# One denominator product per attention half instead of two, in a four-layer graph network on one core

## Chip, core and metric

The kernel runs on one core of a Trainium2 chip. The metric is the device time of one launch in microseconds (us). The kernel before has a median of 4019.16 us over three runs (4017.57 to 4020.96).

## What is computed

There are 16 graphs of 1024 nodes with 256 features, and one 1024x1024 adjacency matrix for all. Each graph goes through three graph-attention layers (4, 1 and 1 heads) and then one transformer block with 8 masked attention heads of width 32 and a feed-forward part. The change touches the attention of the last layer only, cut here to what matters:

```python
def _L3_gnn_ref(x, adj, w_qkv, ...):
    qkv = jnp.einsum('fnc,ck->fnk', x, w_qkv)
    q, k, v = jnp.split(qkv, 3, axis=-1)          # then 8 heads of 32
    scores = jnp.einsum('fnhd,fmhd->fhnm', q, k) / sqrt(32)
    scores = jnp.where(adj > 0, scores, -1e9)
    attn = jax.nn.softmax(scores, axis=-1)
    t = jnp.einsum('fhnm,fmhd->fnhd', attn, v).reshape(F, N, C)
    ...
```

The kernel makes the softmax without a maximum: weight = exp(score) times a 0/1 mask. The numerator is the product of weights and values, the denominator is the sum of the weights over m, and the quotient of the two is the result.

## The kernel before, in words

**Attention of one graph** (function `attention`, lines 1138 to 1461). The 8 heads come in two groups g of four, and the 1024 queries in two halves hf of 512. So a graph has four pairs (g, hf), called attention halves here. Each half has eight steps jt, one for each tile of 128 keys. A step does the following.

- TensorE computes four score tiles of 128 keys x 512 queries, one for each head (line 1417). They land in a ring of four PSUM tiles `sc`.
- ScalarE takes the exponential of each (line 1441) into two tiles `pa` of 128x1024, two heads in each. The ring `pa` has six tiles, which is three steps.
- VectorE multiplies each `pa` tile by the mask (line 1450).
- TensorE multiplies the values by the weights, four heads side by side in four 32-column strips of the array (`quad`, line 1274, called at line 1324). The result accumulates over the eight steps in a PSUM bank, `accs[g, hf][0]`.

**The denominator.** The same `quad` with a tile of ones in place of the values gives the sum over keys, in a second bank `accs[g, hf][1]` (line 1339). To spare TensorE, the weights of several steps are first added elementwise into two tiles `sums` (a ring of two, so one set). With a run of four steps this goes so: at the second step VectorE adds the weights of the first two (line 1301); at the third an accumulating transfer, issued from GpSimd, adds its weights into `sums` (line 1318); at the fourth VectorE adds again (line 1309), and then comes the product of ones. A half thus has two products of ones. In the last graph the run is one: each step has its own product of ones, and nothing is added beforehand.

After the eighth step ScalarE copies both banks (line 1357), TensorE transposes them back, and VectorE divides (lines 1377 to 1397). The four PSUM banks of `r_bank` are shared by all stages; a use gets its bank with its first instruction.

**What orders the work.** Nothing is run as it is written. Every operation is recorded with an assumed duration, the buffers that it reads and writes, and a key. The key comes from the graph's number and from a curve (`KNOTS`) for its stage, moved for some engines by `LEAD`. `Record.schedule` (lines 193 to 310) then fills each engine's queue: of the operations that it takes to be ready it takes the one with the least key, with a surcharge `BIAS` times `SWITCH` for a TensorE operation that changes between the full array and the 32-column strips. `PASS` and `SLACK` are its allowances for the hand-over between engines and for a transfer's landing. The result is a fixed order on each engine. The stages of neighbouring graphs lie interleaved in it: while one graph is in its attention, the next is in its graph layers, whose largest parts are the products at line 951 (full array), at lines 1038 and 1048 (32-column strips) and their weights on VectorE (line 924).

Each engine works through its own order and waits there for what an instruction needs. The transfers that SyncE issues (keys, queries, rows, inputs, outputs) are one queue; the adding transfers are in GpSimd's order, together with its small power operations for the layer norms (lines 499 and 514) and its running sums (lines 544 and 875).

Of the kernel before, what the change touches and what calls it, by code (L numbers as in the profile page):

```python
# [113 lines left out]


WEIGHT = {"pe": 1.0, "dve": 0.3}
PASS = {"pe": 0.156, "act": 0.266, "dve": 0.175, "pool": 0.13, "dma": 0.0}


class Port(float):  # L120
# [3 lines left out]
class Work:  # L124


    def __init__(self, engine, us, emit, key, modes, moved, lands):
        self.engine, self.us, self.emit, self.key, self.modes = engine, us, emit, key, modes
        self.pass_on = PASS[engine]
        self.moved = moved  # L130
# [9 lines left out]
def priority(x):  # L140
# [3 lines left out]
    key = base + knots[k] + (knots[k + 1] - knots[k]) * (at - k)  # L144
    return round(key - (LEAD.get(x.engine, 0.0) if lead else 0.0), 6)


class Record:
# [44 lines left out]
    def schedule(self):  # L193
        for n, x in enumerate(self.work):
# [4 lines left out]
            for y in x.before:  # L199
                y.after.append(x)  # L200
        free = dict.fromkeys(PASS, 0.0)
        queue = 0.0
        future = {e: [] for e in PASS}
        now = {e: [] for e in PASS}
        mode = "full"
# [15 lines left out]
        def turn(x):  # L221

            return BIAS * SWITCH.get((mode, x.modes[0]), 0.0) if x.engine == "pe" else 0.0

        def choose(e):

            at = free[e]
            while future[e] and future[e][0][0] <= at:
                x = heapq.heappop(future[e])[2]
                heapq.heappush(now[e], (x.key, x.n, x))  # L230
            best = None
            for key, n, x in now[e]:
                t = opening(x)
                if t is not None:
                    best = min(best or (1e9,), (max(at, t), key + turn(x), n, x))
            if future[e] and (best is None or future[e][0][0] < best[0]):
                for t, n, x in sorted(future[e]):
                    if opening(x) is not None:
                        t = max(t, at, opening(x))
                        best = min(best or (1e9,), (t, x.key + turn(x), n, x))  # L240
                        break
            return best
# [15 lines left out]
        while True:  # L258
            choices = [(c, e) for c, e in ((choose(e), e) for e in PASS) if c]
            if not choices:  # L260
# [30 lines left out]
            if x.moved:  # L291
                if e == "dma" and queue - at > BEHIND:
                    us = max(us, HELD)
                queue = max(at + (us if e == "pool" else 0.2), queue) + x.moved
                x.pass_on = queue + x.lands + SLACK - (at + us)
            order.append(x)
# [14 lines left out]


BEHIND, HELD = 2.0, 1.35
SLACK = 0.748
KNOTS = {
    "gat0": (-11.844, -10.615, -6.023, -6.927, -4.773, -4.496, -2.083, -5.225, -6.038),
    "gat1": (-1.994, -0.279, 0.283, 0.497, 0.692, 0.622, 0.809, 0.954, 0.61),
    "gat2": (1.323, -0.293, -0.231, 0.287, 0.727, 1.303, 1.532, 1.921, 1.614),
    "beside": (1.385, 3.608, 5.021, -2.136, 7.34),
    "values": (-1.057, -3.755, -2.847, -3.057, -2.059, -1.343, 5.264, -0.6, 1.007),  # L320
    "steps": (-0.497, 1.051, 1.31, 1.573, 1.666, 1.995, 2.455, 2.56, -0.935),
    "feed": (3.891, 3.879, 2.109, 1.26, 2.247, 1.635, -2.072, 2.278, 2.962),
    "last": (3.265, -3.949, 2.052, -2.131, 3.084, -1.607, -0.666, 3.92, 2.042),
}
BIAS = 3.411
LEAD = {"act": 1.749, "dve": -1.422}

SWITCH = {
    ("full", "col4"): 0.137,
# [11 lines left out]
def tt_us(n):  # L341
    return Port((n / 0.96 + 67) / 1000)
# [17 lines left out]
def direct(ctx, tc, flag, x, adj, gat_w, gat_a, w_qkv, ln1_g, ln1_b, ln2_g, ln2_b, w1, b1, w2, b2, out):  # L360
# [3 lines left out]
    NB, N, C = x.shape  # L364
    NT = N // P
# [85 lines left out]
    def pe(us, emit, w, r, modes=("full", "full")):  # L451
        rec.add("pe", us, emit, w, r, modes)
# [4 lines left out]
    def dve(us, emit, w, r):  # L457
        rec.add("dve", us, emit, w, r)
# [4 lines left out]
    def dma(moved, lands, emit, w, r, key=None, us=0.42, engine="dma"):  # L463
        rec.add(engine, us, emit, w, r, key=key, moved=moved, lands=lands)
# [673 lines left out]
    def attention(b, xt, b_mv, b_rstd):  # L1138
# [130 lines left out]
        steps = [(g, hf, jt) for g in range(CT) for hf in range(2) for jt in range(NT)]  # L1269
        pas, accs, sums = {}, {}, {}  # L1270

        def quad(ac, of_head, columns, first, last):
            for r in range(HG):
                nc.tensor.matmul(  # L1274
                    ac.t[r * D3 : (r + 1) * D3, :],
                    columns(r),
                    of_head(r),
                    start=first,
                    stop=last,
                )  # L1280

        def run_of(g, hf):

            return 1 if b == NB - 1 else 4

        rec.stream(b, KNOTS["steps"])
        GROUP = 2
# [1 line left out]
        for n in range(len(steps) + LAG):  # L1289
            m = n - LAG  # L1290
            if m >= 0:
                g, hf, jt = steps[m]
                if jt == 0:
                    accs[g, hf] = [r_bank.new(), r_bank.new()]
                run = run_of(g, hf)
                if jt % run == 1:
                    sums[g, hf] = [r_sums.new() for _ in range(2)]
                    for ss, p0, p1 in zip(sums[g, hf], pas[m - 1], pas[m]):
                        dve(
                            tt_us(2 * HALF),  # L1300
                            lambda: nc.vector.tensor_add(ss.t, p0.t, p1.t),  # L1301
                            [ss],
                            [p0, p1],
                        )
                elif run == 4 and jt % run == 3:
                    for ss, pt in zip(sums[g, hf], pas[m]):
                        dve(
                            tt_us(2 * HALF),
                            lambda: nc.vector.tensor_add(ss.t, ss.t, pt.t),  # L1309
                            [ss],  # L1310
                            [pt],
                        )
                elif jt % run:
                    for ss, pt in zip(sums[g, hf], pas[m]):
                        dma(
                            2.4,
                            2.0,
                            lambda: nc.gpsimd.dma_start(ss.t, pt.t, accum_op=ALU.add),  # L1318
                            [ss],
                            [pt],  # L1320
                            us=1.135,
                            engine="pool",
                        )
                pe(
                    0.8585,
                    lambda: quad(
                        accs[g, hf][0],
                        lambda r: pas[m][r // 2].t[:, r % 2, :],
                        lambda r: va.t[:, jt, (g * HG + r) * D3 : (g * HG + r + 1) * D3],
                        jt == 0,  # L1330
                        jt == NT - 1,
                    ),
                    [accs[g, hf][0]],
                    pas[m] + [va(jt)],
                    ("col4", "col4"),
                )
                if jt % run == run - 1:
                    ss = pas[m] if run == 1 else sums[g, hf]
                    pe(
                        0.8585,  # L1340
                        lambda: quad(
                            accs[g, hf][1],
                            lambda r: ss[r // 2].t[:, r % 2, :],
                            lambda r: ones,
                            jt == run - 1,
                            jt == NT - 1,
                        ),
                        [accs[g, hf][1]],
                        ss,
                        ("col4", "col4"),  # L1350
                    )
# [51 lines left out]
            if n < len(steps):  # L1403
                g, hf, jt = steps[n]
# [302 lines left out]
    def end(b, state):  # L1707
        xt, x3 = state[0], r_x3.new()
        for hf in range(2):
            s = slice(hf * TH, (hf + 1) * TH)  # L1710
            dma(
                1.3,
                1.6,
                lambda: nc.sync.dma_start(x3.t[:, s, :], xt.half(hf)),
                [x3(hf)],
                [xt(it) for it in range(hf * TH, (hf + 1) * TH)],
            )
        hn = attention(b, *state)
        rec.stream(b, KNOTS["last" if b == NB - 1 else "feed"])
        feed(b, x3, hn)  # L1720
# [630 lines left out]
```

## Time and profile before

The profiled execution took 4019.4 us, of which 4017.6 us are the span of the trace.

| quantity | before |
|---|---|
| median of three runs | 4019.16 us |
| profiled execution, its span | 4019.4 us, 4017.6 us |
| TensorE matmuls busy | 3953.2 us |
| VectorE busy | 3620.1 us |
| ScalarE busy | 2660.7 us |
| GpSimd busy | 664.7 us |
| products of ones from `sums` (line 1274) | 960 records, 127.1 us busy |
| adding transfers (line 1318) | 240, each 512 KB, 4.8 us from issue to landing (median) |

Busy time is the time in which the profile shows an instruction of the engine. Matmuls overlap one another in it, so the mean duration of one matmul is not what it takes from TensorE's time; the spacing in the chain of work that ended last is. A matmul instruction of this kernel can appear as two records, so 960 records are 480 instructions, four for each of 120 products. Idle time before an instruction is put down to the event that ended it.

### The profile page before, as it was taken

How to read it: one execution, taken by the hardware profiler on the slowest of the kernel's cores; microseconds unless marked ns; L12 is line 12 of the kernel's file. 1: busy time of each engine (PE TensorE's matmuls, PEld its weight loads, DVE VectorE, ACT ScalarE, POOL GpSimd, SP SyncE). 2: the span in 40 equal slices, each digit the busy share in tenths (PEclk: the TensorE clock that was granted, in tenths of full speed). 3: DMA queues.
4: the chain of work that ended last, by engine and by line, in shares of the span. 5: the costliest groups of instructions: out<-in, count | busy, mean ns of one | idle time of the engine just before them, and what ended most of it. 6: DMA issues, size and time to landing. Idle time of an engine off the chain costs nothing.

```text
span 4017.6 us, 65083 instructions
## 1 busy us (share of the span) xinstructions
PE 3953.2 (98%) x23426; PEld 2331.5 (58%) x23426; DVE 3620.1 (90%) x6134; ACT 2660.7 (66%) x6643; POOL 664.7 (17%) x631
## 2 busy tenths in 40 slices
PE   8999999999999999999999999999999999999998
PEld 4566466564655646566565655646656465564654
DVE  7779999999999999999999999999999999998976
ACT  5467575775757766576675766757578575775676
POOL 0101121211212111121211212112021111211110
PEclk9999999999999999999999999999999999999999
DMA  3164454444645345453454544445444454534552
GB/s 130 31 160 110 117 139 110 114 101 114 144 106 125 91 124 124 112 144 91 113 125 114 138 103 113 105 119 135 110 112 106 114 137 106 131 92 111 125 129 61
DMA packets 228667, 460.66 MB, mean 115 GB/s; under 512 B 24816, under 2 KB 59888, under 8 KB 228336
## 3 DMA queue, kind: packets, MB, share of 16 engines
q1 hardware_dynamic: 193776, 330.58, 29.8%
q0 software_dynamic: 34560, 125.84, 16.3%
q8 instruction: 186, 3.05, 0.3%
q14 instruction: 145, 1.19, 0.1%
HBM read 229.45 MB, written 101.06 MB: 82 GB/s over the span
## 4 chain that ended last, share of the span: by engine, by line
PE 84%; ACT 7%; DVE 5%; issue 2%; DMA 2%; SPq 0%; DVEq 0%; ACTq 0%; POOLq 0%
PE bank L951 20%; PE bank L1274 11%; PE bank L1038 11%; PE sc L1417 10%; PE bank L825 6%; PE bank L1517 5%; PE bank L562 5%; PE bank L1048 5%; PE sc L1188 5%; PE sc L1226 3%; ACT pa L1441 3%; ACT hn L533 1%; DMA sums<-pa 1%; DVE sums L1301 1%; ACT waste L479 1%
## 5 line engine op out<-in xcount | busy, mean ns | idle before, releaser
L1450 DVE TENSOR_TENSOR pa<-pa,mask 128x1024 f32<-128x1024 f32 x1024 | 1227.7, 1220 | 52.8 <-ACT pa L1441 50.0
L1441 ACT ACTIVATE pa<-sc 128x512 f32<-128x512 f32 x2048 | 1099.8, 606 | 197.5 <-PE sc L1417 130.9
L924 DVE SCALAR_TENSOR_TENSOR pt<-row,e,mask 128x512 f32<-128x512 f32 x1472 | 1012.4, 747 | 58.0 <-DMA row<-rd 32.8
L951 PE MATMUL bank<-qb,pt 128*128 128x257 f32 x4096 | 942.1, 381 | 3.3 <-ACT qb L847 1.9
L951 PEld LDWEIGHTS bank<-qb,pt 128*128 128x128 f32 x4096 | 771.0, 190 | 175.3 <-issue 30.2
L1417 PE MATMUL sc<-qs,ks 128*128 128x512 f32 x2048 | 699.3, 449 | 2.7 <-ACT pa L1441 2.6
L1274 PE MATMUL bank<-pa,va 128*32 128x512 f32 x4096 | 515.5, 598 | 0.0
L1417 PEld LDWEIGHTS sc<-qs,ks 128*128 128x128 f32 x2048 | 362.6, 189 | 173.9 <-issue 54.1
L1038 PE MATMUL bank<-pt,qb 128*32 128x512 f32 x3840 | 459.4, 594 | 0.7 <-DVE rec L1094 0.4
L1318 POOL DMA_DIRECT2D sums<-pa x240 | 215.0, 897 | 1385.4 <-ACT pa L1441 356.4
L825 PE MATMUL bank<-w_aug,hT 128*128 128x259 f32 (+1 forms) x1504 | 380.3, 394 | 7.4 <-DVE w_aug L649 3.2
L825 PEld LDWEIGHTS bank<-w_aug,hT 128*128 128x128 f32 x1504 | 274.5, 190 | 136.0 <-ACT qb L847 27.6
L1301 DVE TENSOR_TENSOR sums<-pa,pa 128x1024 f32<-128x1024 f32 x240 | 289.7, 1223 | 56.4 <-PE bank L1274 56.4
L979 ACT ACTIVATE ex<-bank,rec 128x256 f32<-128x256 f32 x256 | 122.0, 476 | 307.6 <-DVE rec L971 307.4
L1309 DVE TENSOR_TENSOR sums<-sums,pa 128x1024 f32<-128x1024 f32 x240 | 291.0, 1223 | 20.0 <-DMA sums<-pa 19.4
L1038 PEld LDWEIGHTS bank<-pt,qb 128*32 128x32 f32 x3840 | 115.8, 109 | 282.4 <-issue 214.3
L1048 PE MATMUL bank<-pt,e 128*32 128x512 f32 x1920 | 251.2, 592 | 0.0
L1274 PEld LDWEIGHTS bank<-pa,va 128*32 128x32 f32 x4096 | 110.4, 109 | 241.8 <-issue 209.6
L1188 PE MATMUL sc<-hTa,wqkv_sb 128*128 128x512 f32 x512 | 244.3, 600 | 0.9 <-ACT pa L1441 0.8
L499 POOL TENSOR_TENSOR rstd<-rstd,neg_half 128x4 f32<-128x4 f32 x94 | 161.7, 1720 | 385.7 <-DVE rstd L491 288.0
L533 ACT ACTIVATE hn<-xh,mv,rstd 128x256 f32<-128x256 f32 x376 | 198.0, 622 | 21.6 <-DVE mv L523 18.7
L1197 ACT CAST hi<-sc 128x512 fp32r<-128x512 f32 x128 | 74.7, 583 | 204.8 <-PE sc L1188 188.0
(153 smaller groups left out, 4673.9 us busy)
## 6 DMA issues: line engine op xcount, KB each, us to landing
sums<-pa POOLq DMA_DIRECT2D x240, 512.0 KB, 4.8
ks<-hl SPq DMA_DIRECT2D x256, 256.0 KB
qs<-hl SPq DMA_DIRECT2D x256, 256.0 KB
row<-rd SPq DMA_DIRECT2D x184, 256.0 KB
hl<-hi SPq DMA_DIRECT2D x128, 256.0 KB
hl<-lo SPq DMA_DIRECT2D x128, 256.0 KB
xh<-in_x_dram SPq DMA_DIRECT2D x32, 512.0 KB
x<-xh SPq DMA_DIRECT2D x32, 512.0 KB
```

What stands on the lines that cost most here:

```text
L825: nc.tensor.matmul(g.t[:, : C + 3 * H], hT.t[:, ct, k * P : (k + 1) * P], w_aug[l][:, ct, :], start=ct == 0, stop=ct == CT - 1,)
L924: lambda: nc.vector.scalar_tensor_tensor(pt.t, row.t, e3[:, 2, jt // TH, h, jt % TH : jt % TH + 1], mask[:, jt, hf * HALF : (hf + 1) * HAL ...
L951: nc.tensor.matmul(g.t[:, : D + 1], pts[jt].t[:, k * P : (k + 1) * P], qb[:, jt, 0, :], start=jt == 0, stop=jt == NT - 1,)
L1038: nc.tensor.matmul(g.t[u * D + d : u * D + d + D3, :], qb[:, j, h + u, d : d + D3], pts[u][j - jt].t, start=j == 0, stop=j == NT - 1,)
L1048: nc.tensor.matmul(gd.t[c : c + D3, :], one(jt + k, h + u).to_broadcast([P, D3]), pts[u][k].t, start=jt == 0, stop=jt == NT - 2,)
L1188: nc.tensor.matmul(sc.t, wqkv_sb[:, ct, c0 : c0 + P], hT.t[:, ct, hf * HALF : (hf + 1) * HALF], start=ct == 0, stop=ct == CT - 1,)
L1274: nc.tensor.matmul(ac.t[r * D3 : (r + 1) * D3, :], columns(r), of_head(r), start=first, stop=last,)
L1301: lambda: nc.vector.tensor_add(ss.t, p0.t, p1.t),
L1309: lambda: nc.vector.tensor_add(ss.t, ss.t, pt.t),
L1417: nc.tensor.matmul(scs[r - r0].t, ks.t[:, r, jt * P : (jt + 1) * P].bitcast(F32R), q.t[:, r, :].bitcast(F32R), start=True, stop=True,)
L1441: lambda: nc.scalar.activation(pt.t[:, v, :], sc.t, AF.Exp, scale=1.0 / math.sqrt(D3)),
L1450: lambda: nc.vector.tensor_mul(pt.t, pt.t, mask[:, jt : jt + 1, i0 : i0 + HALF].to_broadcast([P, 2, HALF]),),
```

## The change

In all graphs but the last the run grows from four steps to all eight (`NT` is 8). At odd steps VectorE adds (at the first of them, two tiles of weights into a new `sums`), at even steps from the second on a transfer adds. After the eighth step there is one product of ones. The constants of the planner are other ones too, so the whole order of the instructions is made anew.

```diff
-PASS = {"pe": 0.156, "act": 0.266, "dve": 0.175, "pool": 0.13, "dma": 0.0}
+PASS = {"pe": 0.184, "act": 0.255, "dve": 0.2, "pool": 0.13, "dma": 0.0}
...
-SLACK = 0.748
+SLACK = 0.962
 KNOTS = {
-    "gat0": (-11.844, -10.615, -6.023, -6.927, -4.773, -4.496, -2.083, -5.225, -6.038),
+    "gat0": (-10.592, -9.852, -9.404, -9.422, -4.685, -5.744, -2.501, -5.476, -8.387),
...
-    "steps": (-0.497, 1.051, 1.31, 1.573, 1.666, 1.995, 2.455, 2.56, -0.935),
+    "steps": (-0.731, 1.092, 1.111, 1.525, 1.942, 1.949, 3.509, 2.697, 0.422),
...
 }
-BIAS = 3.411
-LEAD = {"act": 1.749, "dve": -1.422}
+BIAS = 3.565
+LEAD = {"act": 3.258, "dve": -0.77}
...
         def run_of(g, hf):
 
-            return 1 if b == NB - 1 else 4
+            return 1 if b == NB - 1 else NT
...
-                elif run == 4 and jt % run == 3:
+                elif run > 1 and jt % 2:
                     for ss, pt in zip(sums[g, hf], pas[m]):
                         dve(
                             tt_us(2 * HALF),
```

All eight curves of `KNOTS` are changed, of which two are shown.

## Prediction, made before the changed kernel was run

> **What bounds the kernel now.** I read the page first: busy shares, then the chain of work that ended last.
>
> ```profile
> PE 3953.2 (98%) x23426; PEld 2331.5 (58%) x23426; DVE 3620.1 (90%) x6134; ACT 2660.7 (66%) x6643; POOL 664.7 (17%) x631
> ...
> PE 84%; ACT 7%; DVE 5%; issue 2%; DMA 2%; SPq 0%; DVEq 0%; ACTq 0%; POOLq 0%
> ```
>
> TensorE is busy for all but 64 us and makes 84% of the chain. VectorE, at 90%, is the next bound. The view by stages (span, then busy us of PE, PEld, DVE, ACT, POOL, clock, DMA share) says where TensorE's idle time lies:
>
> ```profile
> 0.00:60.00 60.00, 44.29 (x330) 25.98 (x330) 41.06 (x99) 38.64 (x111) 6.78 (x14) 1.00 0.51 173
> 60.00:120.00 60.00, 50.77 (x382) 23.05 (x379) 54.45 (x125) 21.99 (x55) 4.94 (x6) 0.94 0.18 54
> ...
> 260.00:500.00 240.00, 238.02 (x1415) 134.18 (x1413) 219.70 (x354) 153.94 (x357) 34.75 (x35) 1.00 0.50 117
> 500.00:3000.00 2500.00, 2482.80 (x14691) 1473.67 (x14690) 2309.78 (x3868) 1692.39 (x4263) 439.38 (x410) 1.00 0.48 117
> 3000.00:3700.00 700.00, 696.33 (x4179) 410.60 (x4178) 642.56 (x1086) 466.61 (x1160) 118.09 (x111) 1.00 0.47 113
> 3700.00:3860.00 160.00, 159.56 (x822) 103.78 (x822) 144.25 (x238) 111.57 (x274) 32.01 (x29) 1.00 0.56 132
> ```
>
> From 260 to 3860 us, where all work that the change touches lies, TensorE is idle for 2.0 + 17.2 + 3.7 + 0.4 = 23.3 of 3600 us. The first 120 us hold 24.9 us more. So in the stages concerned TensorE's own work sets the time, and VectorE has 7.6% spare there (2500 less 2309.78 us).
>
> Next, what a product costs TensorE: the chain in order of time, around the middle (start, us on the chain, what, records).
>
> ```profile
> 2013.35 0.93 PE sc L1417 x4
> ...
> 2022.60 3.57 PE bank L1274 x32
> 2026.17 1.13 PE sc L1417 x4
> ...
> 2209.73 2.71 PE bank L1274 x24
> ...
> 2224.45 1.86 PE bank L1274 x16
> ...
> 2238.06 0.99 PE bank L1274 x8
> ```
>
> A quad is 8 records. Four, three and two in a row take 3.57, 2.71 and 1.86 us, so one more in a row costs 0.86 us. One alone takes 0.99, hence 0.13 for going into the 32-column strips. A score group takes 0.93 after a full-array product and 1.13 after a quad, hence 0.20 for coming out. A visit to the strips costs 0.33 us besides its quads.
>
> Last, three views of `sums`: its groups on VectorE (busy, mean ns, then idle before and its releaser), the wait for the transfers (us, times, longest), and the transfers (count, size, median us to landing):
>
> ```profile
> L1309 DVE TENSOR_TENSOR sums<-sums,pa 128x1024 f32<-128x1024 f32 x240 | 291.0, 1223 | 20.0 <-DMA sums<-pa 19.4
> L1301 DVE TENSOR_TENSOR sums<-pa,pa 128x1024 f32<-128x1024 f32 x240 | 289.7, 1223 | 56.4 <-PE bank L1274 56.4
> ```
>
> ```profile
> DVE sums L1309 <- DMA sums<-pa: 19.4, 18, 2.3
> ```
>
> ```profile
> sums<-pa POOLq DMA_DIRECT2D x240, 512.0 KB, 4.8
> ```
>
> VectorE's wait for the adding transfers is small: 18 of 240 additions waited, 19.4 us in all. Its wait of 56.4 us for line 1274 is the second run of a half, which needs the one set of `sums` back from the first run's product.
>
> **What the Trainium skill says.** *TensorEngine Tiling (Array Packing)*, Key Properties: changing the tiling mode drains TensorE. The trace agrees, with the 0.13 and 0.20 us above. *Perfetto Trace Analysis*, Identifying the Most-Contended Engine: matmul busy share is a poor measure, since matmuls are pipelined. I therefore price by spacing on the chain (0.86 us for a quad), not by busy time (127.1 us for 120 products, 1.06 each). *DMA: Bandwidth & Descriptors*, SWDGE vs HWDGE vs iDMA: a transfer that accumulates can only be issued from GpSimd; so the new ones join GpSimd's one order. *SBUF — State Buffer*, SBUF: two separate sides: VectorE operations with two SBUF inputs share a port with GpSimd, exclusively, but only against GpSimd operations that read SBUF. The trace shows transfer issues of 862 to 1182 ns, median 901, while VectorE is 90% busy, mostly with such operations: they are not held long.
>
> **The change, part by part.**
>
> *Products removed.* 15 graphs of 4 halves lose one product each: 60. At 0.86 us that is −51.6 us, all of it on TensorE. I take the price in a row, since the built order has only 4 products of ones standing alone among full-array work before, and 3 after. Alone, a product would save 0.99 + 0.20 = 1.19 us.
>
> *Visits to the strips.* The order of instructions built from both kernels (an order, no times) has 393 visits before and 405 after. 12 x 0.33 = +4.0 us. Net TensorE work: −47.6 us.
>
> *VectorE's additions.* Each addition is two instructions, one for each tile of `sums`. A half had 4 at line 1301 (steps 2 and 6) and 4 at line 1309 (steps 4 and 8). It has 2 (step 2) and 6 (steps 4, 6 and 8) now. Both kinds take 1223 ns: 0 us.
>
> *Transfers.* A half had 4 (steps 3 and 7) and has 6 (3, 5, 7): 120 more. Each costs GpSimd 0.90 us to issue, 108 us in all on an engine busy 17%. On the DMA engines their queue took 16.3% of the span for 240, so 120 more take 8.2%, over a mean load of some 46%. What is moved past is SyncE's queue of keys, queries and rows; VectorE's waits for a row are 32.8 us in total now and may grow. I count 0 on the path: 23.3 us of TensorE idle time in the steady part says that none of these loads is late at TensorE. If the row waits doubled, 33 us of VectorE time would go, against some 190 us that it has spare in the 2500 us stretch alone; only what exceeds that reaches TensorE.
>
> *The wait added.* 360 additions at line 1309 follow a transfer, in place of 240. At the same rate VectorE's wait grows by 9.7 us. Behind the addition in VectorE's order stand masks (line 1450) and the graph layers' weights (line 924), for which TensorE waits in turn. The cover: an issue pair (2 x 0.90) and a landing (4.8) need 6.6 us after the mask. In the built orders, with durations from the trace, VectorE has less than 6.5 us of work between the two in 4 of 240 cases before and in 2 of 360 after. So the rate stays about the same. In GpSimd's order the small power operations now stand behind more issues. VectorE waits for these for 15.7 + 13.1 + 8.9 us today; half as much again is 19 us, within its spare time.
>
> *Waits removed.* The 56.4 us at line 1301: a half now starts its sums once, after the product of the half before, so 60 of 120 starts remain, and I expect half the wait to go, −28 us of VectorE idle. With +10 and +19 above VectorE comes out even. Also a bank: the denominator's accumulator was held from step 4 and is now taken at step 8 only, so three banks are open to the other stages for longer, and TensorE's idle time need not grow.
>
> *The new order.* Other constants move everything. TensorE's idle time outside its work is what they can change: below, 17 us (most of the steady 23.3); above, about the same again as there is, 23 us. I take 0, since cover and waits came out even.
>
> Sum against the profiled execution: 4019.4 − 51.6 + 4.0 = 3971.8 us. That execution lies 0.2 us above the median of the runs, so the forecast for the median is 3972 us. What is late next is still TensorE: VectorE's share rises only to 3620 / 3970 = 91%.
>
> **The rivals.**
>
> *Part of the gain is lost to VectorE.* With less TensorE work per graph, VectorE's share in the steady part goes from 92.4% to 93.5%, and masks come late more often. For: ScalarE and VectorE waits make 12% of the chain already. Against: VectorE's net waits do not grow. If the steady idle time doubles (+23.3), 3995 us.
>
> *More than the removed work.* The bank that is free for longer and the new curves take away most of the steady idle time: 3972 − 17 = 3955 us. For: the shared banks are only four. Against: 23.3 us in 3600 is little to win from.
>
> *Slower: the chain of seven additions is late.* A half's product of ones now hangs on three transfers and four VectorE additions in a row. If the last transfer lands late, TensorE stands in its order before the one product of ones, in each half. It decides from 47.6 / 60 = 0.8 us of stall per half; at the longest wait seen for such a transfer, 2.3 us, it gives 3972 + 138 = 4110 us. Against: eight steps take some 60 us (240 us for a graph with 32 steps, interleaved with other work), and each link needs under 10.
>
> *It does not do what it says.* The removed product was hidden in time when TensorE waited anyway: about 4019 us. Against: 23.3 us of idle time cannot hide 51.6 us.
>
> **How the numbers follow.** Forecast (3962 to 3982) 0.46; part lost (3982 to 4011) 0.22; more (under 3962) 0.18; no effect 0.05; slower 0.09. A measurement of this kernel can tell about 0.2% from no change, 8 us, so faster is under 4011 and sums to 0.86, within is 0.05, slower 0.09. The range leaves out the slower case, no effect, and the far ends of the two neighbours: 3950 to 4005 us.
>
> **What would show it.** Right: 480 records of bank<-sums,ones instead of 960, TensorE busy near 3906 us, its idle time from the second graph to the last near 23 us, 360 transfers landing in about 4.8 us, line 1301 waiting half as long, line 1309 waiting some 30 us. Wrong: TensorE idle before line 1274 released by `sums`, a landing well above 4.8 us, or a score group that costs more than 0.93 us in more places than counted.

## The result, and the profile after

The changed kernel takes 3967.42 us (median of four runs, 3965.86 to 3969.25) against 4020.06 us for the kernel before, a ratio of 0.9868 with a 95% interval of 0.9851 to 0.9885. Timed again later it took 3970.41 us, ratio 0.9875 (0.9859 to 0.9892). The gain is thus 50 to 53 us; 3972 us was forecast. The profiled execution has a span of 3966.4 us, 51.2 us less than before.

The page of the changed kernel, busy shares:

```profile
PE 3915.6 (99%) x22946; PEld 2325.5 (59%) x22946; DVE 3616.0 (91%) x6134; ACT 2659.1 (67%) x6643; POOL 819.1 (21%) x751
```

TensorE has 480 records fewer and is busy for 37.6 us less; its idle time fell too, from 64.4 to 50.8 us. The two together are the 51.2 us. The forecast had split it otherwise: busy near 3906 us and idle time in the steady part near 23 us. As busy time also holds stalls (experiment 1), the sum of the two says more than the split. The view by stages (columns as before) shows where the idle time went:

```profile
260.00:500.00 240.00, 235.66 (x1365) 134.52 (x1364) 222.50 (x345) 150.93 (x344) 41.33 (x40) 0.99 0.59 137
500.00:3000.00 2500.00, 2496.85 (x14598) 1495.33 (x14597) 2348.16 (x3946) 1722.36 (x4338) 565.41 (x504) 1.00 0.58 137
3000.00:3650.00 650.00, 649.33 (x3872) 383.05 (x3874) 605.66 (x1022) 439.88 (x1088) 143.31 (x128) 1.00 0.54 129
3650.00:3810.00 160.00, 156.32 (x810) 103.07 (x803) 143.50 (x241) 111.56 (x284) 36.17 (x35) 1.00 0.65 151
```

In the steady part, from 260 to 3810 us, TensorE is idle for 4.3 + 3.2 + 0.7 + 3.7 = 11.8 of 3550 us, half of before. VectorE's share there is 93.9% in the long stretch (2348.16 of 2500).

The price of a quad on the chain of work is as it was (start, us on the chain, what, records). The chain can be followed back over the last quarter of the span only:

```profile
3397.09 2.71 PE bank L1274 x24
...
3407.91 1.85 PE bank L1274 x16
3411.26 0.99 PE bank L1274 x8
...
3470.79 3.57 PE bank L1274 x32
```

The groups of `sums` on VectorE (busy, mean ns, idle before and releaser), then the wait for the transfers, then the transfers:

```profile
L1309 DVE TENSOR_TENSOR sums<-sums,pa 128x1024 f32<-128x1024 f32 x360 | 433.9, 1215 | 9.8 <-DMA sums<-pa 9.2
L1301 DVE TENSOR_TENSOR sums<-pa,pa 128x1024 f32<-128x1024 f32 x120 | 143.6, 1209 | 0.4 <-PE bank L1274 0.4
```

```profile
DVE sums L1309 <- DMA sums<-pa: 9.2, 5, 4.4
```

```profile
sums<-pa POOLq DMA_DIRECT2D x360, 512.0 KB, 5.0
```

There are half as many additions again that follow a transfer, and they wait for less than before (9.2 instead of 19.4 us). Of the wait of 56.4 us for the product of ones 0.4 us is left. A landing takes 5.0 us for 4.8.

So the sum came out. But the change has two parts, the longer run and eight curves' worth of new constants, and the sum does not say which of them did it. That is what the experiments ask.

### The profile page after: what moved, and what is told of

It is laid out like the page before. It is cut to its first block, busy times and chain, and to the rows that moved or that the text cites. A ratio compares the mean times of both kernels' runs of the same rounds, so it can differ in the third digit from the quotient of the medians.

```text
span 3966.4 us, 64316 instructions
## 1 busy us (share of the span) xinstructions
PE 3915.6 (99%) x22946; PEld 2325.5 (59%) x22946; DVE 3616.0 (91%) x6134; ACT 2659.1 (67%) x6643; POOL 819.1 (21%) x751
## 5 line engine op out<-in xcount | busy, mean ns | idle before, releaser
L1450 DVE TENSOR_TENSOR pa<-pa,mask 128x1024 f32<-128x1024 f32 x1024 | 1225.3, 1215 | 84.2 <-ACT pa L1441 83.0
L951 PE MATMUL bank<-qb,pt 128*128 128x257 f32 x4096 | 952.2, 381 | 3.8 <-ACT rt L897 3.2
L1417 PE MATMUL sc<-qs,ks 128*128 128x512 f32 x2048 | 743.6, 467 | 3.1 <-ACT pa L1441 2.8
L1318 POOL DMA_DIRECT2D sums<-pa x360 | 317.4, 882 | 1124.1 <-DVE pa L1450 324.5
L1274 PE MATMUL bank<-pa,va 128*32 128x512 f32 x4096 | 533.4, 599 | 1.0 <-DVE pa L1450 1.0
L1309 DVE TENSOR_TENSOR sums<-sums,pa 128x1024 f32<-128x1024 f32 x360 | 433.9, 1215 | 9.8 <-DMA sums<-pa 9.2
L499 POOL TENSOR_TENSOR rstd<-rstd,neg_half 128x4 f32<-128x4 f32 x94 | 152.0, 1617 | 794.6 <-DVE rec L971 472.6
L479 ACT ACTIVATE waste<-xh,mv 128x256 f32<-128x256 f32 x376 | 191.6, 510 | 8.2
L514 POOL TENSOR_TENSOR rstd<-rstd,neg_half 128x4 f32<-128x4 f32 x66 | 86.7, 1313 | 496.1 <-DVE rstd L511 488.2
```

What stands on the lines that cost most here:

```text
L951: nc.tensor.matmul(g.t[:, : D + 1], pts[jt].t[:, k * P : (k + 1) * P], qb[:, jt, 0, :], start=jt == 0, stop=jt == NT - 1,)
L1274: nc.tensor.matmul(ac.t[r * D3 : (r + 1) * D3, :], columns(r), of_head(r), start=first, stop=last,)
L1417: nc.tensor.matmul(scs[r - r0].t, ks.t[:, r, jt * P : (jt + 1) * P].bitcast(F32R), q.t[:, r, :].bitcast(F32R), start=True, stop=True,)
L1450: lambda: nc.vector.tensor_mul(pt.t, pt.t, mask[:, jt : jt + 1, i0 : i0 + HALF].to_broadcast([P, 2, HALF]),),
```

## Experiments

Theory: the 60 removed products are TensorE time, 0.86 us each, and everything else comes out even. Rivals: the gain comes from the new constants; or the products lie in time that TensorE would have waited anyway, so that another part brought the gain.

**1. The longer run under the planner's constants of before.**

```diff
 (kernel before)
-            return 1 if b == NB - 1 else 4
+            return 1 if b == NB - 1 else NT
...
-                elif run == 4 and jt % run == 3:
+                elif run > 1 and jt % 2:
```

> The run of eight steps alone, with the planner's constants of before. The built order has 60 quads of ones fewer than before and 436 visits to the 32-column strips (393 before). Theory (the removed products are TensorE time, the constants only order the rest): 4019 - 51.6 + 43 x 0.33 = about 3982 us. Rival (the gain of the changed kernel comes from its new constants): 4011 us or more. Rival (the late chain: the old constants don't provide for three transfers in a row, so TensorE waits for the sums before line 1274): above 4027 us, with that wait in the trace.

Measured: 4296.97 us, ratio 1.0683 (1.0669 to 1.0698). None of the three expectations had this: the kernel does the arithmetic of the changed kernel and is 330 us slower than it. The number lies above the 4011 us of the first rival, but that rival spoke of a gain that is missing, not of a loss of 275 us. The late chain is not it either: VectorE waits 53.3 us for the transfers, but no wait of TensorE for `sums` stands among its larger ones. Its page:

```profile
PE 4081.3 (95%) x22946; PEld 2321.2 (54%) x22946; DVE 3639.2 (85%) x6134; ACT 2671.6 (62%) x6643; POOL 728.0 (17%) x751
```

The same 22946 matmul records are busy for 166 us more, though no work was added (31 more visits to the strips than in the changed kernel, at 0.33 us, are 10 us; a lower clock, see experiment 6, is at most some 18). So here the busy time of matmuls holds stalls. The waits of the weight loads show where to look, though some of such a wait can pass while an earlier product still runs (waiting instruction, releaser: us, times, longest). In this kernel:

```profile
PEld sc L1417 <- ACT pa L1441: 257.5, 508, 2.7
...
PEld bank L1038 <- DVE pt L924: 189.8, 236, 2.3
```

and in the changed kernel:

```profile
PEld sc L1417 <- ACT pa L1441: 67.3, 156, 2.8
...
PEld bank L1038 <- DVE pt L924: 45.3, 115, 1.2
```

TensorE stands before the scores until ScalarE has freed a tile of `sc`, and before the graph layer's products until VectorE has made the weights: 447 us of such waits instead of 113. The work is the same, and it waits more for the other engines; which feature of the order does this, the run does not show.

**2. The new constants under the short run.** The two edited lines of the change are put back in the changed kernel, the constants stay.

> The planner's new constants alone, with the run of four steps as before. 472 visits to the strips in the built order (393 before), all quads of before. Theory: the constants bring nothing by themselves, 4019 + 79 x 0.33 = about 4045 us. Rival (the constants carry a part of the gain whatever the run): below 4011 us.

Measured: 4180.75 us, ratio 1.0391 (1.0377 to 1.0406). The rival falls: the constants bring nothing by themselves, under the short run. The expectation was missed as well, by 136 us: the visits (79 more) are the small part of what an unfit order costs.

**3. The product of ones issued twice, in the changed kernel's own order.**

```diff
+                    def denominator():
+                        for k in range(2 if run == NT else 1):
+                            quad(accs[g, hf][1], ..., lambda r: ones,
+                                 jt == run - 1 and k == 0,
+                                 jt == NT - 1 and (k == 1 or run < NT))
+
                     pe(
                         0.8585,
-                        lambda: quad(...),
+                        denominator,
```

> The changed kernel with each of its 60 products of ones issued twice in a row into the same bank, the planner's duration unchanged, so the order of all else is that of the changed kernel (405 visits). The denominators of 15 graphs are doubled by it. Theory: 60 quads in a row cost 60 x 0.86 = 51.6 us, 3967 + 52 = 4019 us. If a quad cost what its busy share says (1.06 us): 4031 us. If the products lie in time that TensorE has anyway: about 3967 us.

Measured: 4017.68 us (13 runs), ratio 0.9992 (0.9984 to 1.0000): the whole gain is gone. Against the two timings of the changed kernel this is 50.3 and 47.3 us, or 0.84 and 0.79 us for a product. Its page:

```profile
PE 3968.7 (99%) x23426; PEld 2344.7 (58%) x23426; DVE 3625.2 (90%) x6134; ACT 2663.6 (66%) x6643; POOL 802.0 (20%) x751
```

With the order of all else unchanged, 480 records of TensorE cost what the forecast said they would, and nothing hides them.

**4. The changed kernel without the surcharge for changes of tiling** (`BIAS = 3.565` becomes 0).

> The changed kernel with BIAS at 0, so that the planner does not save changes of tiling: 628 visits to the strips in the built order instead of 405. Theory: 223 x 0.33 = 74 us, about 4041 us. If changes of tiling were hidden or cost only the planner's estimate at one end (0.13): 3996 us. If the order without the surcharge also wins idle time, less than 4041 by that, which the idle time of TensorE will show.

Measured: 4328.34 us, ratio 1.0768 (1.0754 to 1.0783), 361 us above the changed kernel; the 223 visits would be 74 of it. As in experiment 1 the waits of the weight loads for ScalarE's exponentials grew (253.8 us). As a price of a visit the run is of no use, since its order is unfit in other ways too.

**5. One constant of the kernel before moved by 5%** (`BIAS` from 3.411 to 3.565).

> The kernel before with one constant moved by 5% (BIAS 3.411 to 3.565), all else as it was; 462 visits to the strips in the built order instead of 393. Theory A (each set of constants fits one program only, and any other order loses overlap): 4019 + 69 x 0.33 = 4042 us at the least, and rather 4100 to 4200 us, like the short run under the new constants. Theory B (constants of before are good near where they are, and fail at the long run because of its transfers): 4019 to 4045 us, no more than the visits.

Measured: 4240.79 us, ratio 1.0550 (1.0536 to 1.0564). Theory B falls, and the loss is even larger than the 4200 us that theory A named. One step of one constant does not map out how narrow the fit is, but it is enough for this: experiments 1, 2 and 4 say nothing against the longer run. Against the kernel with the same arithmetic, the five orders of experiments 1, 2, 4, 5 and 6 that were not found for their program cost it 4 to 10%.

**6. The changed kernel with the planner's allowances of before** (`PASS` and `SLACK` put back, curves kept).

> The changed kernel with the planner's allowances (PASS, SLACK) of before, and the new curves, BIAS and LEAD; 491 visits instead of 405. Theory A (any mismatch loses): 3967 + 86 x 0.33 = 3996 us at the least, rather 4050 to 4250 us, with waits spread over many lines. Theory B (the larger allowance for a landing is what the longer chain needs): the loss stands at line 1309 waiting for transfers and at line 1274 waiting for the sums, by more than the 9.2 and 1.7 us of the changed kernel, and makes most of it.

Measured: 4358.64 us, ratio 1.0840 (1.0825 to 1.0855). VectorE waits 23.2 us at line 1309 for the transfers, 14 us more than in the changed kernel. But ScalarE, whose exponentials need a free weight tile, waits long for the transfers that still read one:

```profile
L1441 ACT ACTIVATE pa<-sc 128x512 f32<-128x512 f32 x2048 | 1084.0, 604 | 709.0 <-DMA sums<-pa 387.0
```

In the changed kernel the same line waits 6.0 us for transfers:

```profile
ACT pa L1441 <- DMA sums<-pa: 6.0, 4, 4.2
```

```profile
L1441 ACT ACTIVATE pa<-sc 128x512 f32<-128x512 f32 x2048 | 1099.7, 602 | 375.4 <-PE sc L1417 263.7 <-DVE sums L1301 63.6 <-DVE rstdz L491 24.9
```

And TensorE's longest wait in this run is that of the values' product for the masked weights, which stood at 1.0 us in the changed kernel:

```profile
PE bank L1274 <- DVE pa L1450: 114.3, 29, 7.9
```

So the loss does not stand where theory B put it, at the additions and the product of ones, but neither is it without a place: as the waits read, the landing of the transfers counts in this order, through the six tiles of `pa`, then the exponentials, the masks and the values' product. Theory A's "spread over many lines" is only half right. A further part is the clock: the mean granted TensorE clock was 0.978 in this run and 0.997 in the changed kernel. An estimate from the two spans, (1 − 0.978) x 4362.3 less (1 − 0.997) x 3966.4, is some 84 of the 391 us, if TensorE had work in all of that time. In experiments 1, 2, 4 and 5 the clock is lower too (0.993, 0.992, 0.989 and 0.991 in the profiled runs), which by the same estimate is 18 to 36 us each. Why it fell is open.

**7. The kernel before, in its own order, without the first of its two products of ones.**

```diff
+                    def denominator():
+                        if run == 4 and jt == 3:
+                            return
+                        quad(...)
...
-    nc.scalar.copy(ot.t, ac[u].t)
+    nc.scalar.activation(ot.t, ac[u].t, AF.Copy, bias=float(u), scale=1.0)
```

> The kernel before, its order kept, with the first of the two products of ones of each half left out in 15 graphs (the denominator then holds the weights of steps 5 to 8 only, plus 1, which the copy of the bank adds so that it is never zero). The 60 quads are gone, and with them what waits for them at line 1301; transfers, additions and the order of all else are those of before; 391 visits for 393. Theory: 4020 - 60 x 0.84 = about 3970 us, which leaves nothing for the rest of the change. If the order of before holds its time elsewhere (a wait takes the place of the product): 3985 us or more. If it gains beyond the product by the freed wait at line 1301: below 3960 us, and then the changed kernel's transfers and order cost that difference.

Measured: 3999.58 us, ratio 0.9940 (0.9927 to 0.9954): 22.5 us, 0.38 us for a product. The second case of the expectation is what happened. TensorE's matmuls are busy for 3926.8 us, 26.4 us less than before, and its idle time is up by 9. Two waits of the weight loads for ScalarE grew by 38 us each: the scores' wait for a free `sc` tile, and at line 825 the wait for `hT`, the input of a graph layer. Here they are

```profile
PEld sc L1423 <- ACT pa L1447: 84.5, 207, 1.2
...
PEld bank L825 <- ACT hT L819: 44.2, 46, 1.9
```

(lines behind the edit are moved by six), and before the edit they were:

```profile
PEld sc L1417 <- ACT pa L1441: 46.5, 98, 1.5
...
PEld bank L825 <- ACT hT L819: 6.3, 18, 0.9
```

The wait at line 1301 fell from 56.4 to 16.3 us, and no gain beyond the product shows for it.

**8. 120 transfers more in the changed kernel's order.** They are plain copies to scratch memory, not adding transfers. (`jt` counts from 0, so `jt == 4` is the fifth step; the odd and even steps in the description of the change are counted so too.)

```diff
+                        def transfer():
+                            nc.gpsimd.dma_start(ss.t, pt.t, accum_op=ALU.add)
+                            if jt == 4:
+                                junk.append(junk.pop(0))
+                                nc.gpsimd.dma_start(junk[0], pt.t)
```

> The changed kernel with 120 more GpSimd transfers of 512 KB (one plain copy of each weight tile of the fifth step into scratch memory, right after its adding transfer, the tile being held until both have landed); the order of all else is that of the changed kernel. As many as the change added. Theory (the added transfers lie beside other work): 3967 to 3975 us. Rival (issue or landing reaches the path): each costs up to its issue of 0.9 us, 4075 us, with waits for the copies at line 1441 or for GpSimd's power operations.

Measured: 3988.80 us, ratio 0.9918 (0.9905 to 0.9932), 18 to 21 us above the changed kernel or some 0.17 us for each. Neither number was right. The median landing of the adding transfers rose from 5.0 to 5.5 us, and VectorE's wait for a row from 33.0 to 47.9 us. So a transfer that the order does not reckon with cost about a fifth of its mean issue time (930 ns) here. Whether the issue, the landing or the tile held for longer costs this is not separated.

**9. 120 of the adding transfers cut to an eighth.**

```diff
+                        w = HALF // 8 if jt == 4 else HALF
...
-    nc.gpsimd.dma_start(ss.t, pt.t, accum_op=ALU.add)
+    nc.gpsimd.dma_start(ss.t[:, :, :w], pt.t[:, :, :w], accum_op=ALU.add)
```

> The changed kernel, its order and all issues kept, with the 120 adding transfers of the fifth step cut to an eighth of their bytes (that step's weights are added for one query in eight only). As much transfer work as the change added is gone from the DMA engines, and these land earlier. Theory (in the order made for them the added transfers cost nothing): 3965 to 3969 us. Rival (what 120 plain copies cost in an order that did not know of them, 21 us, is also what the added transfers cost): 3945 to 3955 us.

Measured: 3978.70 us, ratio 0.9891 (0.9876 to 0.9906); the changed kernel's interval overlaps it, but both forecast ranges were missed. Less data brought no time, and the rival falls as a number: no cost of the bytes shows in the order made for them. But the mean issue became longer (1002 for 882 ns), so what the issues cost is not told by this run, and a gain from the bytes could be hidden behind it. The median landing moved little, from 5.0 to 4.8 us.

**10 and 11. The last graph.** The change leaves its run at one step. Experiment 10 makes it eight there too (`return NT`), experiment 11 two (`return 2 if b == NB - 1 else NT`).

> The changed kernel with the run of eight in the last graph as well: 32 products of ones there become 4, visits 406 for 405. Theory (TensorE sets the last graph's time too, which shows it busy for 120 of 120 us): 3967 - 28 x 0.86 = 3943 us. Rival (in the last graph nothing lies beside the attention, so the product of ones waits for its chain of additions): 3967 us or more, with TensorE idle before line 1274.

> The changed kernel with a run of two steps in the last graph: 16 quads fewer, 32 additions of VectorE more, no transfer there; 405 visits. Theory (in the last graph it was the chain through the transfers that the run of eight lost on, and TensorE sets the time without it): 3967 - 16 x 0.84 = 3954 us. Rival (any addition in the last graph is late, because VectorE has nothing spare that is not in the chain): 3967 us or more.

Measured: 4002.60 us for eight (ratio 0.9956, 0.9942 to 0.9969) and 3990.95 us for two (0.9924, 0.9911 to 0.9938), both slower than the changed kernel, though TensorE has 28 and 16 quads fewer. Both rivals have the time right. The stretch of the last graph in the changed kernel, with eight, and with two, in this order:

```profile
3810.00:3930.00 120.00, 120.00 (x713) 49.85 (x715) 94.79 (x115) 85.03 (x187) 7.07 (x5) 1.00 0.36 96
```

```profile
3810.00:3930.00 120.00, 102.33 (x398) 38.98 (x398) 100.28 (x111) 70.17 (x156) 20.18 (x22) 0.91 0.76 170
```

```profile
3810.00:3930.00 120.00, 115.49 (x555) 46.55 (x557) 111.87 (x124) 80.06 (x175) 6.51 (x5) 1.00 0.39 102
```

With two, VectorE is busy for 112 of 120 us; it is the bound there, even without a transfer. With eight, fewer matmuls come in the same stretch (398 for 713), VectorE is busy for 100 us of it, and the granted clock was 0.91. The sign that the rival named is hardly there: from 3800 us on TensorE's weight loads wait 38.0 us for exponentials before the scores and 21.2 us for masks, but 3.4 us for `sums` before the product of ones. ScalarE stands 18.5 us there for transfers that still read a weight tile. So the path through the held `pa` tiles, as in experiment 6, fits better than the late sum; this is read from the waits and not tested. No version was found that beats the changed kernel. (The constants were not searched anew for either.)

**12. The changed kernel again**, as the base of experiments 3, 8 and 9.

> The changed kernel itself, timed in more rounds, as the base for the experiments that keep its order (a second product of ones, 120 more transfers, 120 smaller transfers). Theory: 3967 us, ratio 0.987, so that the smaller transfers are really some 10 us slower and not faster. If it lies at 3975 us or more, the smaller transfers are no different from it.

Measured: 3970.41 us, ratio 0.9875 (0.9859 to 0.9892). It lies between the two cases of the expectation: the smaller transfers are not faster, and whether they are 8 us slower or the same is open.

## Why the prediction was right, step by step

- *Products removed, −51.6 us.* Right. Experiment 3 puts 47 to 50 us on the 60 products in the changed kernel's order, with nothing else moved. The price by spacing on the chain, 0.86 us, was the right one; busy time would have said 1.06. The page *Perfetto Trace Analysis* of the Trainium skill (Identifying the Most-Contended Engine) says that the busy share of matmuls is no good measure of how close a kernel is to its limit, because pipelined matmuls look smaller in the trace. The warning holds here, but the direction is the other one: busy time was larger than the spacing, and in experiment 1 the same records were busy for 166 us more.
- *Visits to the strips, +4.0 us.* The count was right, since it is that of the built order. The price of 0.33 us was not measured by itself: the runs with more visits lost far more than the visits account for.
- *VectorE's additions, 0.* Right: 1215 ns after, 1223 before, 480 of them in both.
- *Transfers, 0.* No cost shows in this order as far as bytes go (experiment 9, with its longer issues as a reservation); as a general price 0 is wrong (experiment 8). The wait for rows stayed at 33.0 us.
- *The wait added, +10 us of VectorE's time.* It fell by 10 us instead. The step kept the rate of waits although its own count of short covers fell from 4 of 240 to 2 of 360; the waits counted went the same way, from 18 to 5. The waits for GpSimd's power operations were forecast to go from 37.7 to 57 us and fell to 26.8 us (20.6 + 4.8 + 1.4).
- *Waits removed, −28 us of VectorE's time.* The size was off: 56.0 of 56.4 us went. The prediction had itself read this wait as that of the second run of a half, and no second run is left. It seems to matter little: experiment 7 freed 40 us of the same wait, and TensorE gained less than the product alone.
- *The new order, 0.* Here the sum was right and the argument was not. The step bounded the order by TensorE's idle time, −17 to +23 us, and took 0 "since cover and waits came out even". The bound was unsound: as experiment 1 shows, TensorE's stalls stand in its busy time too, and in the trace of before its weight loads already waited 46.5 us for exponentials at line 1417 and 38.3 us for the weights at line 1038. For the same reason 23.3 us of idle time could not rule out that a removed product was hidden, nor that transfers were late. And an order is worth far more than that: the changed program under other constants takes 4297, 4328 or 4359 us, and the program before under a constant moved by 5% takes 4241 us. Nor does the removal pay in any order: in that of before 22.5 of 51.6 us come back. That the rest needs an order laid out for the shorter TensorE work is the likely reading; the freed bank and the other parts of the change were not tried alone. That the constants of the change fit its program could not be read from the trace of before, so it is luck that this term came out near nothing. The rival that should have been written is "the order does not fit, +4 to +10%", in place of the late chain, for which the changed kernel shows 1.7 us of wait at the product of ones, once.

What stays open: which property of an order makes it fit. Common to experiments 1, 2, 4, 5 and 6 is that TensorE waits for ScalarE's exponentials before the scores (122 to 258 us at the weight loads, against 47 and 67 us in the two fitting orders) and that the granted clock is lower. That is where part of the time goes, not why the planner lays it out so. Nor was the run of four steps given new constants of its own, so how much of the 1.3% a better order alone could have brought is not known.

## What to carry to other kernels

Price a removed matmul by the spacing on the chain of the engine that binds, and check it by putting the work back twice in the new kernel's order: here the one gave 0.86 us and the other 0.79 to 0.84. Taking the work out of an order that was not made without it gave 0.38 us. In a kernel whose order comes from a planner with fitted constants, a structural edit and its constants can't be judged apart: the edit alone lost 7% here and the constants alone 4%, and only the pair gained 1.3%. Read the waits of weight loads beside those of matmuls, since here a TensorE that is "95% busy" took 330 us longer for the same work.

## What was not expected of the hardware

GpSimd's small running sum (line 875, 128x12 elements) takes 1064 ns on average before and 1975 ns after, with the same operands, while the issue of a transfer stayed at 897 and 882 ns. Of the 154 us that GpSimd's busy time grew by, these 64 instructions are 58, and the added transfers 102. The lines of before, of the changed kernel and of experiment 8, where line 875 is line 876:

```profile
L875 POOL TENSOR_TENSOR sum_e<-sum_e,e 128x12 f32<-128x12 f32 x64 | 68.1, 1064 | 135.5 <-ACT e L836 135.5
```

```profile
L875 POOL TENSOR_TENSOR sum_e<-sum_e,e 128x12 f32<-128x12 f32 x64 | 126.4, 1975 | 96.6 <-ACT e L836 96.6
```

```profile
L876 POOL TENSOR_TENSOR sum_e<-sum_e,e 128x12 f32<-128x12 f32 x64 | 65.1, 1018 | 81.0 <-ACT e L837 80.9
```

Experiment 8 keeps the order of the changed kernel and still has 1018 ns, and experiments 3 and 9, which keep it too, have 2002 and 2102 ns, so the order of the instructions alone does not set this time. *SBUF — State Buffer* of the Trainium skill (SBUF: two separate sides) names a port that GpSimd operations reading SBUF share with VectorE operations of two SBUF inputs. How often the two meet there could differ from run to run; no run here tests it, and no instruction is seen to wait for these sums in the changed kernel.
